# One plan between two scans: preparation beside the back stage, tiles of successive stages in shared slabs of SBUF

## The chip, the cores and the metric

The kernel runs on one core of a Trainium2 chip. The metric is device time in microseconds (us), the median of three runs. Engines are named as in the profile: PE is TensorE, DVE is VectorE, ACT is ScalarE, POOL is GpSimd, and SP is the engine whose queue issues all DMAs of this kernel.

## The reference

A batch of 8 images of 96 channels and 64 x 64 positions passes two layers. The first is a group norm, then a selective scan ("VSS") block with a residual; the second is linear attention and a quantized feed-forward block on 4096 tokens of 96. Cut to what matters:

```python
xh = layernorm(gn(x))                      # per position over 96 channels
xi, z = split(xh @ in_proj_w.T + in_proj_b)    # 192 and 192 channels
xi = silu(depthwise_conv3x3(xi) + conv_b)
xs = stack([xi_hw, xi_wh, flip(xi_hw), flip(xi_wh)])    # 4 directions k
dts, Bs, Cs = split(einsum('bkdl,kcd->bkcl', xs, x_proj_w), [6, 22])
delta = softplus(einsum('bkrl,kdr->bkdl', dts, dt_proj_w) + dt_proj_b)
# scan over 4096 positions, 16 states per channel:
h = exp(delta_t * A) * h + (delta_t * u_t) * B_t ;  y_t = sum_n h * C_t
y = layernorm(sum of the 4 directions, turned back) * silu(z)
x = x + y @ out_proj_w.T + out_proj_b
t = tokens(x)
t = t + linear_attention(layernorm(t))     # (q k^T) v without softmax: k^T v first
t = t + ffn(layernorm(t))                  # 96 -> 384 -> 96, operands rounded to fp8
```

## The kernel before

Images are worked in four pairs. For a pair the stages are:

- **project**: load x, statistics, group norm and layer norm, the input projection. Its output goes to three padded tiles `y` in SBUF (T = 0 and 1 hold 128 channels of either image, T = 2 the other 64 of both), and `zs` (silu of z) to DRAM. 16 chunks of 512 positions, 8 for each image.
- **convolve**: the 3 x 3 convolution from `y` to `xi`; T = 0 and 2 on DVE (lines 473 and 476), T = 1 on PE with diagonal weights (line 483), then Silu on ACT.
- **prepare**: for 2 orders (row-major, column-major), 8 chunks and 2 directions: x_proj on PE (line 543), dt_proj (line 555), softplus on ACT, `du` on DVE (line 560), and delta in three bf16 parts `dp` (ACT, DVE line 571, POOL line 576). `us`, `du`, `dl`, `bs` and `cs` are written to DRAM. Column-major chunks are first copied by POOL (line 535).
- **scan**: 128 steps of 128 positions (32 for each of the 4 directions), loaded from DRAM; it writes `ys`. A separate, hand-ordered program that the change leaves alone.
- **back**: 16 units. Load `ys` (tile `yk`), add directions (line 866 on DVE and POOL), turn by PE (line 880), layer norm (line 899), gate with `zs`, output projection, residual to `ta`, its normalized form to `tns`; keys and values (line 931) and their products summed in the bank `pm` (line 938). `ta` and `tns` are stored to DRAM as `t1` and `tn`. After the last unit the 96 x 96 attention matrix `hm` of each image is made.
- **tail**: 16 units. Load `tn` and `t1`, apply `hm` (line 985), layer norm, two fp8 products (lines 993 and 1004) and the output (line 1012). It needs `hm`, so it can't begin before back's last unit.

`norm` (lines 357, 361, 365) is the layer norm that project, back and tail share: a centering matmul into a bank of the ring `hold`, a square, a matmul into a bank of `q`, Ln and Exp on ACT, and a multiply on DVE which frees the `hold` bank. Nearly all ACT instructions are recorded at line 332 and all these DMAs at line 351.

**The order** of these stages is not that of the code. Every operation is added to a `Plan` with its engine, an assumed cost, the names that it reads and writes, the rings of tiles or PSUM banks that it needs a place of, and a `rank`. `Plan.run` then plays a schedule: for each engine it takes, among the operations that could begin within 0.1 us of the earliest, the one of least rank, and emits the earliest of these. A DMA is played on one queue of 0.23 MB/us. The instructions of each engine stand in the program in that order, and an engine runs them in order. Rings `unit` and `chunk` with three places limit how many units of back or tail and how many chunks of project are under way. Two plans run between scans: back of the last pair with project of the next (banks: 3 `q`, 2 `hold`, 2 `py`, and `pm`), then tail of the last pair with convolve and prepare of the next (3 `q`, 1 `hold`, 4 `big`). Their pools of SBUF are opened and closed with the plan. Before the first scan there is no back or tail, after the last one nothing else.

Constants are loaded ahead of everything, at the head of SP's queue, and `decay_weights()` (from line 285 on: an Exp, splits on DVE, four 128 x 6144 products at line 317, and DMAs to and from DRAM) stands between the first two plans.

Of the kernel before, what the change touches and what calls it, by code (L numbers as in the profile page):

```python
# [19 lines left out]
DIM = 96  # L20
# [17 lines left out]
HQ = TC // 4  # L38
NE = 24
# [12 lines left out]
class Plan:  # L52
# [9 lines left out]
    def __init__(self):  # L62
        self.ops, self.wrote, self.read = [], {}, {}
        self.free, self.left, self.tiles, self.home = {}, {}, {}, {}
        self.unit = None
# [7 lines left out]
    def add(self, engine, cost, emit, reads=(), writes=(), new=(), rank=0.0, kind=None, size=0.0):  # L73
        i = len(self.ops)
        after = set()
        for name in reads:
            after.update(self.wrote.get(name, ()))
            self.read.setdefault(name, []).append(i)
# [78 lines left out]
def vss_attn_ffn(ctx: ExitStack, tc: tile.TileContext, a: dict):  # L157
# [19 lines left out]
    gmat = load("gmat", [DIM, DIM])  # L177
    c96 = load("c96", [DIM, DIM])
    j96 = load("j96", [DIM, DIM])
    hmask = load("hmask", [DIM, DIM])  # L180
    j192 = const.tile([DIM, DIM], F32, name="j192")
    nc.sync.dma_start(j192, a["j192"][0:DIM, 0, 0:DIM])


    nw = load("nw", [DIM, 1])
    nb = load("nb", [DIM, 1])
    inb = const.tile([128, 2], F32, name="inb")
    nc.sync.dma_start(inb, a["inb"][:, 0])
    convw = load("convw", [128, 2, 9])
    convb = load("convb", [128, 2])  # L190
    dtb = load("dtb", [128, KD, 2])


    xwd = dram.tile([128, KD, 3, 76], F32, name="xwd", bufs=1)
    with tc.tile_pool(name="xprep", bufs=2) as wp:
        xw = wp.tile([128, KD, 3, 76], F32, name="xw", bufs=1)
        for k in range(KD):
            for g in range(2):
                xg = wp.tile([128, 3, 2 * NS], F32, name="xg")
                nc.sync.dma_start(xg, a["xw"][k, :, g, :, 0:32])  # L200
                for b in range(2):
                    o = 32 * g + NS * b
                    nc.vector.tensor_copy(
                        xw[:, k, :, o : o + NS].rearrange("p t (n z) -> p t n z", z=2),
                        xg[:, :, NS * b : NS * b + NS].rearrange("p t (z n) -> p t n z", z=2),
                    )
            nc.sync.dma_start(xw[:, k, :, 64:76], a["xw"][k, :, 0, :, 32:44])
        nc.sync.dma_start(xwd, xw)

    def cut(name, v, *rest):  # L210

        t = const.tile([DIM, 2, *rest], F32, name=f"c_{name}")
        nc.sync.dma_start(t[:, 0], v[0:DIM, 0])
        nc.sync.dma_start(t[0:32, 1], v[DIM:128, 0])
        nc.sync.dma_start(t[32:DIM, 1], v[0:64, 1])
        return t
# [5 lines left out]
    inz = const.tile([128, 2], F32, name="inz")  # L222
    for o in (0, 64):
        nc.sync.dma_start(inz[o : o + 64, 0:1], a["inb"][0:64, 1, 0:1])
    nc.sync.dma_start(inz[0:64, 1:2], a["inb"][64:128, 1, 0:1])
    nc.sync.dma_start(inz[64:128, 1:2], a["inb"][0:64, 1, 1:2])
    outb = load("outb", [DIM, 1])
    wkv = load("wkv", [DIM + 1, 2 * DIM])
    wqT = load("wqT", [DIM, DIM + 1])
    wff = load("wff", [DIM, DIM])  # L230
    bff = load("bff", [DIM + 1, DIM], part=slice(DIM, DIM + 1))


    dsum = const.tile([DIM, 2], F32, name="dsum")
    nc.vector.tensor_reduce(dsum, ds, mybir.AxisListType.X, ALU.add)
    ad = dram.tile([3, KD, DI, NS], BF16, name="ad", bufs=1)
    awd = dram.tile([KD, 128, 48 * 128], BF16, name="awd", bufs=1)

    blk = const.tile([128, 16], F32, name="blk")
    nc.sync.dma_start(blk, ident[0:16, 0:16].unsqueeze(1).to_broadcast([16, 8, 16]))  # L240


# [4 lines left out]
    with tc.tile_pool(name="wprep", bufs=1) as wp:  # L247
        w1 = wp.tile([DIM, HID], F32, name="w1")
        nc.sync.dma_start(w1, a["w1T"])
        nc.vector.tensor_copy(w1q, w1, saturate=False)  # L250
        w2 = wp.tile([128, 3, DIM], F32, name="w2")
        nc.sync.dma_start(w2, a["w2T"])
        nc.vector.tensor_copy(w2q, w2, saturate=False)
        b1 = wp.tile([128, 3], F32, name="b1")
        nc.sync.dma_start(b1, a["b1"])
        b18 = wp.tile([128, 3], F8, name="b18")
        nc.vector.tensor_copy(b18, b1, saturate=False)
        nc.vector.tensor_copy(b1q, b18)
        b2 = wp.tile([DIM, 1], F32, name="b2")
        nc.sync.dma_start(b2, a["b2"])  # L260
        b28 = wp.tile([DIM, 1], F8, name="b28")
        nc.vector.tensor_copy(b28, b2, saturate=False)
        nc.vector.tensor_copy(b2q, b28)
# [18 lines left out]
    def decay_weights():  # L282

        with tc.tile_pool(name="aprep", bufs=1) as wp:
            am = wp.tile([128, KD, 2, NS], F32, name="am")
            nc.sync.dma_start(am, a["alog"])
            nc.scalar.activation(am, am, AF.Exp)  # L290
            nc.vector.tensor_scalar(am, am, -1.0, None, ALU.mult)
            for i in range(3):
                ap = wp.tile([128, KD, 2, NS], BF16, name=f"ap{i}")
                nc.vector.tensor_copy(ap, am)
                if i < 2:
                    nc.vector.tensor_tensor(am, am, ap, ALU.subtract)
                for k in range(KD):
                    nc.sync.dma_start(ad[i, k, 0:128], ap[:, k, 0])
                    nc.sync.dma_start(ad[i, k, 128:DI], ap[0:64, k, 1])
            mask = wp.tile([128, 16], F32, name="mask")  # L300
            for p in range(3):
                nc.sync.dma_start(
                    mask[32 * p : 32 * p + 32],
                    ident[0:16, 0:16].unsqueeze(1).to_broadcast([16, 2, 16]),
                )
            for p in range(2):
                nc.sync.dma_start(mask[96 + 16 * p : 112 + 16 * p], ident[0:16, 0:16])
            for k in range(KD):
                ac = wp.tile([128, NE * NS], BF16, name="ac", bufs=2)
                for i, rows, n in ((0, slice(0, 96, 2), 6), (1, slice(1, 96, 2), 6), (2, slice(96, 128), 4)):  # L310
                    nc.sync.dma_start(
                        ac[rows],
                        ad[i, k].rearrange("(s c) n -> s (c n)", s=8).unsqueeze(0)
                        .to_broadcast([n, 8, NE * NS]),
                    )
                aw = wp.tile([128, 48, 16, 8], BF16, name="awp", bufs=2)
                nc.vector.tensor_tensor(
                    aw,
                    ac.rearrange("p (c n) -> p c n", n=8).unsqueeze(2).to_broadcast([128, 48, 16, 8]),
                    mask.unsqueeze(1).unsqueeze(3).to_broadcast([128, 48, 16, 8]), ALU.mult,  # L320
                )
                nc.sync.dma_start(awd[k], aw.rearrange("p c m n -> p (c m n)"))

# [30 lines left out]

    def norm(P, n, src_, read, dst, written, new, hold, rank, **kw):

        mm(P, 0.9, lambda: nc.tensor.matmul(P["ncp" + n][:DIM], c96, src_(), start=True, stop=True),  # L357
           (read,), ("ncp" + n,), (("ncp" + n, hold),), rank)
# [4 lines left out]
           ("nsq" + n,), ("nvp" + n,), (("nvp" + n, "q"),), rank)  # L363
# [5 lines left out]
    def project(P, pair, zs, ybuf, p1):  # L369

        pad = [t.rearrange("p (h w) -> p h w", w=HH + 2) for t in ybuf]
        for T in range(3):
            for edge in (pad[T][:, 0], pad[T][:, HH + 1], pad[T][:, :, 0], pad[T][:, :, HH + 1]):
                P.add("POOL", 0.4, lambda edge=edge: nc.gpsimd.memset(edge, 0.0), (), (f"edge{T}",))
        winT = p1.tile([DIM, 2 * DI], F32, name="winT")
# [4 lines left out]
        ring(P, p1, "xt", 2, [DIM, L])  # L380
        ring(P, p1, "zt", 2, [128, 2, F])
        P.ring("chunk", [None] * 3)
# [4 lines left out]
        for b in range(2):  # L387
            mv, gm, gd, gv, gr = stat[b]
            X, S = f"xt{pair}.{b}", f"stat{b}"
            k0 = b * 10 / 20  # L390
            for c in range(0, NCH, 2):
                cs = slice(c * F, c * F + 2 * F)
                dma(P, 0.4, lambda X=X, cs=cs: P[X][:, cs], lambda b=b, cs=cs: x[2 * pair + b, :, cs],
                    (), (f"{X}#{c}", f"{X}#{c + 1}"), ((X, "xt"),), k0 - 1)
            for c in range(NCH):
                dve(P, 0.67, lambda b=b, c=c, X=X: nc.vector.bn_stats(
                    bst[b][:, c, :], P[X][:, bass.ts(c, F)]), (f"{X}#{c}",), (f"{S}#{c}",), (), k0)
# [4 lines left out]
                P[g][:DIM, 0:1], gmat, mv[:, 0:1], start=True, stop=True), (S + "a",), (g,), ((g, "q"),), k0)  # L402
# [6 lines left out]
                P[v][:DIM, 0:1], gmat, gv, start=True, stop=True), (S + "v",), (v,), ((v, "q"),), k0)  # L409
# [7 lines left out]
            for c in range(NCH):  # L417
                cs = bass.ts(c, F)
                rank = k0 + (c + 2) / 20
# [4 lines left out]
                    P[X][:, cs], P[X][:, cs], gm, gr, ALU.subtract, ALU.mult),  # L424
                    (S + "r", S + "m"), (xc,), (), rank)
                norm(P, n, lambda X=X, cs=cs: P[X][:, cs], xc, lambda X=X, cs=cs: P[X][:, cs], (xc,), (),
                     "hold", rank)
                dve(P, 0.66, lambda X=X, cs=cs: nc.vector.tensor_scalar(
                    P[X][:, cs], P[X][:, cs], nw, nb, ALU.mult, ALU.add), (), (xc,), (), rank)
# [3 lines left out]
                    P[pm], winT[:, 0:128], P[X][:, cs], start=True, stop=True),  # L433
# [391 lines left out]
    def back(P, pair, ys, us, zs, t1, tn, tmp, psm):  # L825
        tns = ring(P, tmp, "tns", 3, [DIM + 1, F])
        for i, t in enumerate(tns):
            nc.gpsimd.memset(t[DIM : DIM + 1], 1.0)
# [358 lines left out]
```

## Time and profile before

| | |
|---|---|
| median of 3 runs (lowest, highest) | 10556.45 us (10539.96, 10565.98) |
| the profiled execution: its time, its span | 10552.56 us, 10550.8 us |
| busy in the span: PE, DVE, ACT, POOL | 7647.5, 9068.0, 6962.8, 7996.9 us |
| DMA | 2095.56 MB, mean 199 GB/s |
| scan steps begin and end, first scan | 638.9 us, 2414.6 us |
| scan steps begin, second, third, fourth scan | 3228.7, 5821.8, 8417.2 us |
| last scan step ends | 10192.6 us |

The profile is one execution. "Busy" is the time in which an engine had an instruction under way; a row of a group gives line, engine, operation, what it writes and reads, the count, the busy time and the mean of one. A stage's table gives the same busy times for one stretch, then the share of PE's clock that was granted, the busy share of the 16 DMA engines, and what they moved. Between scans of different pairs the program passes through stages with different limits, so the stretch has to be chosen before the row is read.

### The profile page before, as it was taken

What the parts mean: (1) busy time and instruction counts of PE and PEld (TensorE: products, weight loads), DVE (VectorE), ACT (ScalarE), POOL (GpSimd) and SP (SyncE); (2) the same over time, 40 slices, a digit from 0 to 9 for tenths busy, and PEclk for the clock granted to TensorE, in tenths of its full rate; (3) what the DMA queues carried; (4) which work ended last, traced back from release to release, by engine and by line L of the source; (5) the groups of instructions that cost most, each with busy time, mean ns of one, the idle gap of its engine ahead of it and who ended that gap; (6) DMA issues with size and microseconds to landing.
All of it is one profiled execution on the core that took longest, in us unless ns stands there. A gap on an engine that the chain in (4) does not pass through costs nothing. (4 is left out here: it accounts for less than half of the span.)

```text
span 10550.8 us, 377529 instructions
## 1 busy us (share of the span) xinstructions
PE 7647.5 (72%) x163328; PEld 5376.1 (51%) x163328; DVE 9068.0 (86%) x6702; ACT 6962.8 (66%) x12201; POOL 7996.9 (76%) x2802
## 2 busy tenths in 40 slices
PE   6766666668985676666987666776698666666678
PEld 2235555555324565555532555665553255555554
DVE  3689999996668999999566999999857699999985
ACT  3567777775566777776656677777665577777754
POOL 0579999992148999999124999999812599999961
PEclk8679999999878989999987889889897799989999
DMA  2787888879478888787947888888775778787885
GB/s 75 203 212 212 217 214 214 217 212 203 123 192 213 214 214 216 211 218 192 210 131 194 213 214 215 214 214 215 195 181 159 192 213 216 213 215 215 214 200 138
DMA packets 1597751, 2095.56 MB, mean 199 GB/s; under 512 B 407603, under 2 KB 1048116, under 8 KB 1592500
## 3 DMA queue, kind: packets, MB, share of 16 engines
q1 hardware_dynamic: 1596084, 2071.39, 75.6%
q8 instruction: 1283, 21.02, 0.9%
q14 instruction: 384, 3.15, 0.1%
HBM read 1606.82 MB, written 464.01 MB: 196 GB/s over the span
## 5 line engine op out<-in xcount | busy, mean ns | idle before, releaser
L743 DVE TENSOR_TENSOR_SCAN h<-da,dbu 128x774 f32<-128x774 f32 x4096 | 7026.7, 1759 | 128.2 <-POOL dbu L707 43.4
L707 POOL TENSOR_TENSOR dbu<-dut,bc 128x1536 f32<-128x1536 f32 x2048 | 7083.5, 3601 | 60.8 <-DMA dm<-dl 42.4
L732 ACT ACTIVATE da<-da 128x768 f32<-128x768 f32 x4092 | 3260.2, 797 | 1985.0 <-PE da L725 1970.1
L725 PE MATMUL da<-dm,aw 128*128 128x128 bf16 x24576 | 2282.4, 235 | 2329.8 <-DVE h L743 2089.6
L725 PEld LDWEIGHTS <-aw 128*128 128x128 bf16 x24576 | 1793.6, 104 | 2574.9 <-issue 2287.7
L761 PE MATMUL yp<-h,cw 128*32 128x48 f32 x131072 | 2902.4, 238 | 78.7 <-issue 65.7
L761 PEld LDWEIGHTS yp<-h,cw 128*32 128x32 f32 x131072 | 2410.2, 154 | 527.2 <-issue 207.0
L661 ACT ACTIVATE cw<-bc,blk 128x512 f32<-128x512 f32 x2048 | 1472.6, 720 | 81.5 <-DMA dm<-dl 81.5
L576 POOL TENSOR_TENSOR dp<-rest,dp 128x512 bf16<-128x512 f32 x384 | 456.8, 1194 | 665.3 <-ACT dp L332 620.0
L866 POOL TENSOR_TENSOR yd<-yk 128x768 f32<-128x768 f32 x64 | 125.6, 1962 | 779.6 <-DMA yk<-ys 407.1
L535 POOL COPY u<-xi 128x512 f32<-128x512 f32 x96 | 205.3, 2153 | 534.4 <-ACT xi L332 502.1
L555 PE MATMUL big<-S,dtw 12*128 12x512 f32 x768 | 521.1, 805 | 120.2 <-ACT d L332 96.0
L769 ACT ACTIVATE yev<-yp 128x384 f32<-128x384 f32 x1024 | 505.6, 494 | 64.5 <-PE yp L761 64.2
L571 DVE TENSOR_TENSOR rest<-d,dp 128x512 f32<-128x512 f32 x384 | 345.0, 904 | 207.6 <-ACT dp L332 161.2
L332 ACT ACTIVATE dp<-rest 128x512 bf16<-128x512 f32 x384 | 239.2, 628 | 304.6 <-DVE rest L571 303.5
L704 ACT COPY dbu<-h 128x12 f32<-128x12 f32 x1984 | 409.3, 206 | 0.0
L555 PEld LDWEIGHTS big<-S,dtw 12*128 12x128 f32 x768 | 157.7, 231 | 439.0 <-ACT d L332 225.7
L332 ACT ACTIVATE small<-hold 96x512 f32<-96x512 f32 x192 | 113.8, 593 | 313.5 <-PE hold L357 295.8
L560 DVE TENSOR_TENSOR du<-d,u 128x512 f32<-128x512 f32 x192 | 210.1, 1102 | 118.9 <-ACT d L332 118.9
L880 PEld LDWEIGHTS py<-ident,yd 128*96 128x96 f32 x2048 | 245.4, 165 | 91.2 <-issue 83.9
L476 DVE SCALAR_TENSOR_TENSOR xi<-y,c_convw,xi 128x2048 f32<-128x2048 f32 x128 | 290.3, 2347 | 0.0
L483 PE MATMUL big<-y,diag 128*128 128x512 f32 x576 | 260.2, 615 | 18.3 <-ACT xi L332 12.5
(122 smaller groups left out, 6009.5 us busy)
## 6 DMA issues: line engine op xcount, KB each, us to landing
dut<-du SPq DMA_DIRECT2D x2048, 384.0 KB
dm<-dl SPq DMA_DIRECT2D x1024, 288.0 KB
dl<-dp SPq DMA_DIRECT2D x256, 384.0 KB
dm<-dl SPq DMA_DIRECT2D x1024, 96.0 KB
ys<-yev SPq DMA_DIRECT2D x1024, 96.0 KB
du<-du SPq DMA_DIRECT2D x256, 256.0 KB
bc<-cs SPq DMA_DIRECT2D x512, 128.0 KB
bc<-bs SPq DMA_DIRECT2D x512, 128.0 KB
```

What stands on the lines that cost most here:

```text
L332: "ACT", cost, lambda: nc.scalar.activation(dst(), src_(), func, **kw),
L555: mm(P, 1.0, lambda pq=pq, k=k, T=T, S=S: nc.tensor.matmul(P[pq], dtw[64:76, k, T], P[S][64:76], start=True, stop=True), (S, "dtw"), (pq,) ...
L571: dve(P, 0.88, lambda rest=rest, d=d, dp=dp, w=w: nc.vector.tensor_tensor(w(rest), w(d), P[dp][:, :, 0], ALU.subtract), (d, dp + "#0"), (r ...
L576: P.add("POOL", 1.24, lambda rest=rest, dp=dp, w=w: nc.gpsimd.tensor_tensor(P[dp][:, :, 2], w(rest), P[dp][:, :, 1], ALU.subtract), (rest, ...
L661: nc.scalar.activation(cw[i % 2][:, :, :, m, :].rearrange("p z j t -> p (z j) t"), bc[i][:, 1].rearrange("p z (j t) -> p (z j) t", j=NB), ...
L704: nc.scalar.copy(start, segs(hs[s - 1][:, :, r])[:, :, :, 1 if back else TC])
L707: nc.gpsimd.tensor_tensor(segs(t)[:, :, :, 1:], dut[g].unsqueeze(1) .to_broadcast([128, 2, NI, TC]), bc[s // NB][:, 0, :, bass.ts(c % NB, ...
L725: nc.tensor.matmul(e[:, i], aw[k, r][:, i, z, :], dm[s // 2][:, NI * r + i, bass.ts(c % 2, TC)], start=True, stop=True,)
L732: nc.scalar.activation(e, e, AF.Exp)
L743: nc.vector.tensor_tensor_scan(hs[s][:, w, r][:, d], da[p % 3][:, o : o + W6][:, d], dbu[4 * s + r][:, w][:, d], 0.0, ALU.mult, ALU.add,)
L761: nc.tensor.matmul(y[32 * q : 32 * q + 32, 2 * NE * i : 2 * NE * i + 2 * NE] .rearrange("p (j r i) -> p i j r", j=2, r=NR), w[:, z, :, t], ...
L769: nc.scalar.activation(yev[s][:, :, o : o + 8, :].rearrange("p j i e -> p i j e"), y[:, 0 : 16 * NE].rearrange("p (i j e) -> p i j e", j=2 ...
```

## The change

- `decay_weights` and the loads of constants become rows of the first plan (function `weights`, with ranks); what used to be read freely (`c96`, `nw`, `inb` and so on) becomes a name that an operation reads. The four products move from DVE to POOL.
- The two plans between scans become one. Its banks are 3 `q`, 2 `hold`, 2 `py` and `pm`; before the first scan 4 `q` and 4 `hold`. The x_proj product and the PE part of convolve take a bank of `py` (`hold` before the first scan), dt_proj one of `q`.
- Ranks are rescaled: project 0 to 0.22, convolve to 0.28, prepare from 0.24 to 1, back 0 to 0.65, tail 0.54 to 0.65.
- A `Slab` is one SBUF tile that stages cut up in turn: project's tiles and then `xi` in A1, the padded `y` and then prepare's tiles in A2 (A3, after the weights, before the first scan). While `P.also` is set, each operation added reads that slab's name, and `gate_off` adds a row that writes it, so the plan puts the next user after it. That row emits no instruction.
- Tail takes its tiles from back's `yk` and `yd`. After the last scan, `ta` and `tns` stay in SBUF, and tail reads them there.
- Before the first scan five chunks of project may be under way (was three), with 10 `small` tiles (was 8). With back, `small` has 5 (was 6, and 4 for tail).

```diff
-    gmat = load("gmat", [DIM, DIM])
+    later = []
+    def lay(out_, in_, rank, name, after=()):
+        later.append((out_, in_, rank, name, after))
+    gmat = load("gmat", [DIM, DIM], -0.9)
...
+    class Slab:
+        def __init__(self, pool, name, size):
+            self.all, self.at = pool.tile([128, size], F32, name=name), 0
...
+    def weights(P, wp):
+        P.also = "A3"
+        for out_, in_, rank, name, after in later:
+            dma(P, 0.1, lambda out_=out_: out_, lambda in_=in_: in_, after, (f"w_{name}",), (), rank)
...
-                nc.vector.tensor_tensor(
-                    aw,
+            pool(14.0, lambda n=n, w=w: nc.gpsimd.tensor_tensor(
...
-        P.ring("chunk", [None] * 3)
+        P.ring("chunk", [None] * (3 if beside else 5))
...
-            k0 = b * 10 / 20
+            P.also = f"A1.{b}"
+            k0 = FRONT * b / 2
...
+    def gate_off(P, name):
+        P.add("SP", 0.0, lambda: None, (), (name,), rank=-9)
...
-                        start=(t == 0), stop=(t == 8)), (f"diag#{t}",), (n,), ((n, "big"),), -2 + h)
+                        start=(t == 0), stop=(t == 8)), (f"diag#{t}", "edge1", *[f"pad1#{j}" for j in range(NCH)]), (n,), ((n, "py" if beside else "hold"),), first)
...
-                rank = (o * NCH + c) / 16
+                rank = PREP + (1 - PREP) * (o * NCH + c) / 16
...
-                           (un[T], "xw"), (pt,), ((pt, "big"),), rank)
+                           (un[T], "xw"), (pt,), ((pt, "py" if beside else "hold"),), rank)
...
-                           (S, "dtw"), (pq,), ((pq, "big"),), rank)
+                           (S, "dtw"), (pq,), ((pq, "q"),), rank)
...
-            rank = i / 16
+            rank = BACK * i / 16
...
+            if kept is None:
+                dma(P, 0.2, lambda b=b, cs=cs: t1[b, :, cs], lambda ta=ta: P[ta], (ta,), (f"t1.{b}.{c}",), (), rank)
+                dma(P, 0.2, lambda b=b, cs=cs: tn[b, :, cs], lambda to=to: P[to][0:DIM], (to,), (f"tn.{b}.{c}",), (), rank)
...
-            rank = i / 16
+            rank = TAIL + i / 16 * (TAIL_END - TAIL) if kept is None else 1 + i / 16
...
+            if new and old:
+                psum = banks(P, st, q=3, hold=2, py=2)
+            elif new:
+                psum = banks(P, st, q=4, hold=4)
+            else:
+                psum = banks(P, st, q=3, hold=2, py=2)
+            ring(P, tmp, "small", 5 if old else 10, [DIM, F])
...
+                spare = back(P, pair - 1, old["ys"], old["us"], old["zs"], old["t1"], old["tn"], tmp, psum, kept)
+                tail(P, pair - 1, old["t1"], old["tn"], spare, kept)
+            if new:
+                for b in range(2):
+                    gate_off(P, f"A1.{b}")
+                A1.at = 0
+                xi = [A1.tile([128, L]) for T in range(3)]
+                convolve(P, xi, ybuf, tmp, bool(old))
...
+                prepare(P, A2, xi, new["us"], new["dl"], new["du"], new["bs"], new["cs"], bool(old))
+                P.also = None
+            P.run(table)
```

## The prediction

> **What bounds the kernel now.** I read the span by stage first, because the page's shares average stages with different limits. The four scans take 1776 us each (scan steps L743 from 638.9 to 2414.6 us, and so on); POOL and DVE are busy 1768 and 1757 us of that. Their code isn't touched. What the change can move is the rest, 3446 us: one stage before the first scan (639), three between scans (814, 816, 818) and one after the last (358). Rows of the stage table: interval and length, then busy us (and instructions) of PE, PEld, DVE, ACT, POOL, then granted clock, DMA share, GB/s.
>
> ```profile
> 0.00:638.90 638.90, 427.00 (x714) 136.75 (x715) 342.12 (x349) 305.16 (x499) 194.04 (x142) 0.75 0.57 152
> 2414.60:3228.70 814.10, 687.68 (x2186) 299.05 (x2187) 504.83 (x643) 479.48 (x780) 226.19 (x174) 0.82 0.72 179
> ...
> 10192.60:10550.80 358.20, 296.56 (x1472) 165.65 (x1472) 189.38 (x328) 143.32 (x258) 53.91 (x38) 0.93 0.69 160
> ```
>
> A middle stage is two plans, one after the other. Cut in slices of 27 us it has four regimes with different limits:
>
> ```profile
> 2523.10:2550.20 27.10, 27.10 (x126) 16.05 (x125) 15.96 (x24) 17.59 (x27) 5.04 (x2) 1.00 1.03 233
> ...
> 2740.20:2767.30 27.10, 27.10 (x65) 11.96 (x64) 27.10 (x13) 7.66 (x12) 0.00 (x0) 1.00 0.09 39
> ...
> 2848.70:2875.80 27.10, 26.11 (x40) 7.65 (x39) 13.03 (x21) 16.75 (x29) 7.62 (x6) 0.63 0.64 174
> ...
> 3120.00:3147.10 27.10, 23.35 (x35) 6.65 (x34) 16.58 (x17) 16.01 (x29) 16.73 (x14) 0.66 0.87 223
> ```
>
> Back beside project: PE without a gap. Convolve: PE and DVE full, DMA at 39 GB/s, ACT idle. Prepare beside tail: nothing full, PE at clock 0.63. Prepare alone: DMA 0.87 at 223 GB/s. So PE and DMA are each the limit in turn, and each is idle in the other's turn.
>
> A busy PE overstates its work: a record lasts until the pipeline drains, so its work is the distance between starts. From the timeline of PE:
>
> ```profile
> 2567.34 1.88 PE L899 MATMUL q<-g,j 96*96 96x512 f32 x4
> 2569.06 1.02 PE L432 MATMUL q<-xt,winT 96*128 96x512 f32 x2
> ...
> 2574.15 0.50 PE L938 MATMUL pm<-kv 128*96 128x96 f32 x4
> 2574.49 0.84 PE L931 MATMUL q<-c_wkv,tns 97*128 97x192 f32 x4
> 2575.17 1.04 PE L880 MATMUL py<-ident,yd 128*96 128x128 f32 x8
> 2576.05 1.93 PE L899 MATMUL q<-g,c_woT 96*96 96x512 f32 x4
> ```
>
> 512 columns of f32: 1.72/4 = 0.43 us a record, two records a matmul; L880 0.88/8 = 0.11; L931 0.68/4 = 0.17; L938 0.34/4 = 0.085. Work of a middle stage at full clock: a back unit 32 x 0.11 + 12 x 0.43 (L899) + 8 x 0.17 + 8 x 0.085 + 4 x 0.43 (norm) = 12.5 us, 16 units 200; project 16 x 10 x 0.43 = 69; convolve 144 x 0.43 = 62; prepare 384 x 0.43 = 165; tail at most 16 x (6 x 0.43 + 6 x 0.38) = 78, with 0.38 the length of an L993 record. Together 574 of the 814 us.
>
> **What the Trainium skill says.** "TensorE: Matmul & The Clock Gate", Part 1: PE runs at half clock until it has been busy for some 3.4 us and falls back when idle. The trace agrees: clock 1.00 where PE has no gap, 0.63 in prepare, where eight L543 records in a row take 6.61 us (0.83 each, not 0.43). "Perfetto Trace Analysis", Optimization Strategy: where the most contended engine changes over time, interleaving the regimes can help; that is this change, and the slices above are that case. "ScalarE: Activation LUTs", What ACT_TABLE_LOAD costs: about 1283 ns and a drain of about 1380; the trace shows 1283 ns loads, no drain as a row of its own. "SBUF — State Buffer", Who interferes with whom: a DVE instruction with two SBUF inputs contends with one on POOL that reads SBUF. The trace fits: L535 takes 2.87 us in the first stage, 1.93 in the middle ones. I read what moves from the order in which the changed kernel's instructions stand.
>
> **First stage: -115 us.** Its parts now:
>
> ```profile
> 34.00:185.00 151.00, 101.63 (x168) 35.37 (x168) 37.84 (x78) 90.08 (x131) 0.00 (x0) 0.81 0.21 57
> 185.00:230.00 45.00, 32.67 (x72) 14.17 (x72) 26.14 (x4) 1.12 (x2) 0.00 (x0) 0.89 0.45 167
> 230.00:308.00 78.00, 54.64 (x104) 20.96 (x104) 77.53 (x37) 23.29 (x38) 31.63 (x1) 0.76 0.18 59
> 308.00:615.00 307.00, 235.80 (x352) 64.37 (x352) 188.30 (x197) 183.41 (x319) 149.87 (x120) 0.68 0.87 223
> ```
>
> (1) Ahead of these lie 34 us in which SP issues constants, some 0.45 us each, before x. Now winT, swap and x stand first, so statistics start at about 6: -28. The constants still cost SP the same; they stand before the zs stores, and the last row of inz, which Silu needs, is near place 72: 72 x 0.45 = 32 us, earlier than the first Silu now (60). (2) Project, 151 us: DVE waits 101 us for ACT's normalization there, with two hold banks and three chunks in flight. With four and five it can fall to PE's 102 or stay; I take 125: -26. The 20 table loads of this stage become 12. (3) The decay weights, 45 us between two plans (four products L317, 26.14 us on DVE, and their DMAs), move to POOL beside project: -45. Costed on POOL by L707 (3.565 us for 1536 columns): 6144 columns 14.3, four 57 us; at 1.5 times that (the L535 ratio) 86. Cover: POOL has nothing else before the first u copy (276 us now). The awd stores stand among the zs stores on SP; a late product holds these, then the two zt buffers, then ACT; and prepare's tiles lie in the weights' slab A3, so prepare can't begin before the last awd store. If that is late, this gain is lost. (4) Convolve: part of image 0 goes before project's end; 62 us of DVE work remain after it where 78 are now: -16. (5) Prepare stays at 307 us (DMA). Between -70 and -140.
>
> **A middle stage: -66 us.** Ahead of the first prepare matmul PE now has all of project (69), convolve (62) and about 8 of 16 back units (100): 231 us. Start-up as now: PE worked about 36 of the first 54 us (slices at 2414 and 2441), so 18 lost. After project, DVE has some 48 us of convolve while PE has 72, then Silu. Some 20 us more lost: the first prepare matmul at about 270 (now about 378), 250 to 300. From there PE has at most 8 x 12.5 + 165 + 78 = 343, DVE 323 of 524, ACT in the same proportion 325 of 527 (455 us of activations and 56 loads; 44 now, so 15 us more). None decides. DMA does: SP's order moves 140 MB, 43 before the first us store of prepare, 97 after. Rates seen: 194 GB/s from prepare's start to its end now (76 MB in 394 us; 175 while tail runs beside it), 229 with prepare alone, up to 260 for ys loads. I take 218: 445 us. With first stores 8 us after the matmul and the scan's start-up unchanged at 27 (from the last rest L571 to the first scan step): 270 + 8 + 445 + 27 = 750, against 816. The convolve's DMA hole and the tail's slow stretch are what is gained. Ends: 200 GB/s gives 790, 240 GB/s 710. Costed at nothing: the P.also reads, which are rows of the plan and emit nothing; one more SP DMA; the boundary between the two plans (PE idle 6 of 27 us in the slice at 2713), inside the 18 and 20 lost. Next late: with prepare behind project in PE order, the SP queue. Each store waits at its head for POOL's dp (63.7 us of such waits now in 370), and behind it now wait back's yk loads, so back's start waits for prepare.
>
> **Last stage: -28 us.** Back's part (242 us, PE busy 217) is unchanged but for the 64 t1 and tn DMAs, which nothing waits for until tail. Tail:
>
> ```profile
> 10435.00:10550.80 115.80, 79.14 (x200) 28.51 (x200) 61.65 (x150) 62.03 (x112) 19.87 (x19) 0.87 0.27 82
> ```
>
> With one hold bank a unit's L357 starts only after the previous unit's L365: starts at 10443.67, 10451.15 and 10459.15 in the timeline, 7 to 8 us a unit, while ACT needs 62/16 = 3.9. Two banks and no reload: 5 us a unit, 80 for 107, and a few us at the boundary. Between -10 and -40.
>
> **Sum.** -115 - 3 x 66 - 28 = -341 from 10552.6 (span 10550.8 and 1.8 around it): 10212. The median of the three runs is 4 us higher, so I say 10215. Under 0.3% (32 us) a measurement here can't tell from no change.
>
> **Rivals.** A: DMA doesn't gain; stores at the head of SP's queue hold the loads, and the second part runs at today's 194 GB/s: 97/0.194 = 500, stage 805. With the first stage at -80 and the last at -15: 10552 - 80 - 33 - 15 = 10424. For it: SP's waits above, and both plans were paced by their order rather than by an engine. The case that slab tiles depend on each other, so that nothing overlaps, lands near: middle stages 0, 10552 - 115 - 28 = 10409; against it, the instructions' waits are fewer than before on every engine. B: everything fits; 240 to 250 GB/s and PE at full clock: 97/0.25 = 388, stage 693, -123 each: 10552 - 115 - 369 - 28 = 10040. C, slower: PSUM. Prepare's 96 softplus inputs had four banks of their own; now they share three q banks with back and tail, about 96 + 48 + 96 = 240 uses after the first prepare matmul. If a use holds its bank h us, this part takes 80h. At h = 6.4 a middle stage is 270 + 512 + 35 = 817, no gain; at 7.0 three stages lose 3 x 49 = 147 and eat the other gains, the point from which it decides; at 8, 270 + 640 + 35 = 945 and 10552 - 143 + 387 = 10796. Now a use is a matmul and an activation, 2 to 3.5 us, but ACT is in order and its longest wait inside prepare was 5.4 us.
>
> **How the numbers follow.** My case 0.55, A (with no overlap) 0.25, B 0.14, C 0.06. Range 10050 to 10440: it takes in A, nearly all of B, and leaves out C. Faster 0.94, same 0.01, slower 0.05.
>
> **What would show it.** First scan step near 524 (now 639); scans 1776 as before; middle stages 710 to 790 with no slice under 60 GB/s after the first 200 us, PE clock over 0.8 in prepare, the q users' waits short; tail's L357 starts 5 us apart at the end. It is wrong if middle stages stay over 800, if ACT or PE wait long for q banks, or if POOL's decay products hold the zs stores.

## The result, and the profile after

The changed kernel took **10456.25 us** (median of 4 runs, 10433.23 to 10467.46) against 10561.22 for the kernel before (median of 4): ratio 0.9902, interval 0.9887 to 0.9917. It is faster by about 1%; the prediction had 10215 and a range that began at 10050 and ended at 10440. The sign was right, the size was not: less than a third of the gain came.

The stage table says where it is missing (columns as before: interval, length, busy us and instructions of PE, PEld, DVE, ACT, POOL, then granted clock, DMA share, GB/s):

```profile
0.00:571.20 571.20, 422.44 (x714) 134.00 (x715) 339.47 (x340) 294.78 (x491) 225.81 (x152) 0.73 0.63 170
2348.50:3158.60 810.10, 707.73 (x2186) 302.13 (x2187) 489.98 (x644) 495.60 (x792) 216.57 (x172) 0.83 0.71 180
10116.10:10463.50 347.40, 299.56 (x1472) 165.12 (x1472) 191.75 (x329) 143.32 (x258) 57.19 (x34) 0.93 0.61 128
```

| stage (us) | before | predicted | after |
|---|---|---|---|
| first | 638.9 | 524 | 571.2 |
| middle, three | 814.1, 816.4, 818.2 | 750 | 810.1, 813.7, 810.1 |
| last | 358.2 | 330 | 347.4 |

First -68, the middle ones -4, -3 and -8, last -11: -93, and the four scans 6 us more in this execution (span 10463.5, was 10550.8). Of the 241 us between 10215 and 10456, some 184 are in the middle stages. Four slices of a middle stage, at the places that match those shown for the kernel before:

```profile
2402.50:2429.50 27.00, 27.00 (x102) 14.09 (x101) 15.19 (x24) 19.08 (x32) 3.77 (x2) 1.00 1.13 243
...
2564.50:2591.50 27.00, 27.00 (x65) 11.65 (x64) 25.86 (x14) 7.90 (x12) 0.00 (x0) 1.00 0.05 16
...
2672.50:2699.50 27.00, 23.07 (x43) 9.12 (x44) 13.35 (x16) 18.46 (x30) 9.83 (x8) 0.66 0.82 217
...
3077.50:3104.50 27.00, 23.03 (x33) 5.96 (x32) 14.96 (x27) 18.61 (x30) 7.52 (x5) 0.56 0.57 153
```

Back beside project is as before. Convolve still has a hole in DMA. What was to be new stands in the third and fourth row: prepare beside back, then beside tail. PE is at clock 0.66 and 0.56 there, busy for 23 of 27 us, while DMA is at 0.82 and then 0.57 and DVE, ACT and POOL are far from full. So no engine is full at its full rate; PE's time is nearly filled, at little more than half its rate.

Cut at the first prepare matmul (L594 starts at 2628.9), the stage falls into the two parts of the prediction:

```profile
2348.50:2628.50 280.00, 250.25 (x1095) 129.57 (x1096) 185.45 (x209) 157.86 (x240) 27.82 (x30) 0.94 0.68 155
2628.50:3135.50 507.00, 455.38 (x1076) 170.67 (x1074) 295.75 (x432) 331.99 (x542) 177.74 (x138) 0.79 0.73 191
```

First part 280 us, predicted 270 (250 to 300). Second part, up to the end of the last `rest` (L622), **507 us, predicted 453** (8 to the first stores and 445 of DMA), at 191 GB/s where 218 was taken. That is the miss: 54 of the 60 us by which a middle stage is longer than 750.

### The profile page after: what moved, and what is told of

Same layout as the page of the kernel before. It is cut to its first block, busy times and chain, and to the rows that moved or that the text cites. A ratio compares the mean times of both kernels' runs of the same rounds, so it can differ in the third digit from the quotient of the medians.

```text
span 10463.5 us, 377190 instructions
## 1 busy us (share of the span) xinstructions
PE 7723.3 (74%) x163328; PEld 5391.4 (52%) x163328; DVE 9031.7 (86%) x6692; ACT 6996.6 (67%) x12229; POOL 8006.9 (77%) x2799
## 5 line engine op out<-in xcount | busy, mean ns | idle before, releaser
L627 POOL TENSOR_TENSOR A<-A 128x512 bf16<-128x512 f32 x384 | 469.4, 1226 | 960.3 <-ACT A L287 940.3
L287 ACT ACTIVATE A<-A 128x512 bf16<-128x512 f32 (+2 forms) x809 | 486.2, 619 | 235.3 <-DVE A L622 229.9
L606 PE MATMUL q<-A 12*128 12x512 f32 x768 | 517.5, 786 | 57.2 <-ACT A L287 50.7
L622 DVE TENSOR_TENSOR A<-A 128x512 f32<-128x512 f32 x384 | 338.6, 887 | 206.0 <-ACT A L287 193.5
L586 POOL COPY A<-A 128x512 f32<-128x512 f32 x96 | 143.0, 1501 | 364.8 <-ACT A L287 318.7
L606 PEld LDWEIGHTS q<-A 12*128 12x128 f32 x768 | 147.3, 223 | 368.0 <-ACT A L287 209.0
L611 DVE TENSOR_TENSOR A<-A 128x512 f32<-128x512 f32 x192 | 188.4, 989 | 149.1 <-ACT A L287 148.6
L1073 POOL TENSOR_TENSOR yk<-yk,yd 96x512 f32<-96x512 f32 x64 | 89.7, 1404 | 294.4 <-DVE yd L1071 240.9
L937 PE MATMUL py<-ident,yd 128*96 128x128 f32 x2048 | 284.9, 291 | 24.7 <-DVE yd L923 11.2
L524 DVE SCALAR_TENSOR_TENSOR A<-A,c_convw,A 128x2048 f32<-128x2048 f32 x128 | 299.6, 2380 | 0.2
```

Source lines behind the costliest of these rows:

```text
L287: "ACT", cost, lambda: nc.scalar.activation(dst(), src_(), func, **kw),
L606: mm(P, 1.0, lambda pq=pq, k=k, T=T, S=S: nc.tensor.matmul(P[pq], dtw[64:76, k, T], P[S][64:76], start=True, stop=True), (S, "dtw"), (pq,) ...
L627: P.add("POOL", 1.24, lambda rest=rest, dp=dp, w=w: nc.gpsimd.tensor_tensor(P[dp][:, :, 2], w(rest), P[dp][:, :, 1], ALU.subtract), (rest, ...
L937: nc.tensor.matmul(o, P[yd][:, k, j, DIM * g : DIM * g + DIM], ident, start=(k + j == 0), stop=(k + j == 4),)
```

## The experiments

Two questions: what makes the second part long, and what lengthens the first stage. Stages are separated by scans, which nothing here touches, so an edit that acts in one stage is read in that stage. All are edits of the changed kernel except one; lengths are in us, "middle" is the mean of three, and the ratio is to the kernel before, with its interval.

| run | first | middle | last | median | ratio |
|---|---|---|---|---|---|
| after, first profile | 571.2 | 811.3 | 347.4 | 10456.25 | 0.9902 (0.9887, 0.9917) |
| after, again (c2) | 573.4 | 806.4 | 352.9 | 10460.06 | 0.9914 (0.9897, 0.9932) |
| e1, one ACT table | 570.6 | 793.3 | 345.7 | 10397.62 | 0.9851 (0.9836, 0.9866) |
| e2, 76 rows | 542.8 | 771.2 | 343.9 | 10314.41 | 0.9776 (0.9761, 0.9790) |
| e3, banks | 565.5 | 824.2 | 344.7 | 10492.26 | 0.9941 (0.9924, 0.9957) |
| e4, decay on DVE | 553.7 | 797.2 | 344.0 | 10422.91 | 0.9871 (0.9853, 0.9888) |
| e5, *before* with 76 rows | 638.3 | 794.6 | 355.9 | 10491.96 | 0.9947 (0.9932, 0.9962) |
| e6, 76 rows, DVE, tail banks | 516.8 | 768.8 | 365.3 | 10305.07 | 0.9771 (0.9757, 0.9786) |
| e7, 64 rows | 552.4 | 785.3 | 343.8 | 10364.98 | 0.9829 (0.9814, 0.9843) |
| e8, 128 rows, DVE | 519.6 | 755.7 | 347.2 | 10246.16 | 0.9705 (0.9688, 0.9721) |
| e9, 76 rows, DVE, one table | 512.8 | 749.0 | 343.9 | 10219.04 | 0.9683 (0.9664, 0.9701) |
| e10, 76 rows, DVE, more DMA | 535.5 | 776.7 | 346.9 | 10322.27 | 0.9776 (0.9759, 0.9793) |
| e11, 76 rows, DVE, POOL queue | 543.9 | 787.4 | 349.9 | 10361.61 | 0.9811 (0.9790, 0.9833) |
| e13, 76 rows, same order | 543.2 | 771.3 | 342.2 | 10310.73 | 0.9774 (0.9758, 0.9790) |
| e14, order of e8, 12 rows | 551.2 | 796.9 | 343.8 | 10429.98 | 0.9886 (0.9862, 0.9909) |

**The spread first.** 

> The changed kernel as it is, once more, beside the kernels below on their chip. Expected: 10456 us within 20, middle stages 810 to 814. It serves to read the stage lengths of this group against each other; a spread of more than 10 us in a middle stage between this profile and the first one would mean that stage differences of that size in single profiles carry nothing.

The same program gives middle stages of 801 to 814 us in two profiles; its second part was 495 us in the first middle stage of c2, at clock 0.81. Differences of 10 us in single profiles of kernels with 12 rows are therefore not read. e4 and e14, with 797 us, are such kernels too; the execution profiled was the fastest of their four, some 30 us below their medians.

**1. PE's clock in dt_proj.** dt_proj (L606) multiplies 12 rows of `S` by 12 rows of weights, where x_proj (L594) uses 128. These are the contraction rows: those over which the products are summed. Feeding it more rows with zero weights computes the same and takes the same number of columns.

```diff
+        dve(P, 0.8, lambda: nc.vector.memset(dtw[0:64], 0.0), (), ("dtwz",), (), -1)
...
-                            P[pq], dtw[64:76, k, T], P[S][64:76], start=True, stop=True),
+                            P[pq], dtw[0:76, k, T], P[S][0:76], start=True, stop=True),
```

> The changed kernel with dt_proj (L606) contracting over 76 rows of S instead of 12, the 64 more weight rows zero; same count, columns and result. Theory 'half clock': 12 rows count as little activity for the clock gate; with 76 PE's clock in the second part of a middle stage rises from some 0.77 to over 0.9 and the stage falls to 740-780. Theory 'table loads', 'PSUM banks' or 'SP queue', or a clock that only follows time busy: clock and stage as now, 805-815.

The middle stages fell by 40 us against the first profile after (35 against c2) and the whole by 142. The planner had moved some neighbours, since the zeroing is a row of the plan. So e13 issues the zeroing beside the load of the weights, and PE, ACT, POOL and SP keep the changed kernel's order row for row; e14 goes the other way, from the 128-row kernel below back to 12 rows with nothing else moved.

```diff
-        dma(P, 0.1, lambda: dtw[64:76], lambda
+        dma(P, 0.1, lambda: nc.vector.memset(dtw[0:64], 0.0) and dtw[64:76], lambda
```

> The changed kernel with 76 rows in the dt projection and the zeroing of the weights issued beside their load, so that PE, ACT, POOL and SP keep the changed kernel's order row for row. If the rows are the cause: as with 76 rows before, middle stages 765 to 775, first 540 to 548, total 10305 to 10335. If the planner's other order was the cause: middle 800 to 814, total 10440 to 10465.

```diff
-                            P[pq], dtw[:, k, T], P[S], start=True, stop=True),
+                            P[pq], dtw[64:76, k, T], P[S][64:76], start=True, stop=True),
```

> The kernel with decay products on DVE and 128 rows (middle stages 756, first 520, total 10246), with the contraction put back to 12 rows and every instruction left in its place, the zeroing too. If the rows are the cause: middle 795 to 812, first 548 to 558, total 10390 to 10435, clock in the second part 0.79 to 0.82. If the order was: middle 750 to 762, total 10240 to 10260.

The rows alone decide: e13 equals e2, and e14 gives back all three middle stages, 756 to 797. Matmuls whose rows were left alone got shorter as well. L1046, tail's first matmul, in the second part of the changed kernel and then of e13 (count, busy us, mean ns):

```profile
L1046 PE MATMUL q<-tns,hm 97*96 97x512 f32 x32 | 25.3, 894 | 0.4 <-ACT yd L287 0.4
```

```profile
L1046 PE MATMUL q<-tns,hm 97*96 97x512 f32 x32 | 19.6, 703 | 0.4 <-ACT yd L287 0.4
```

So it is the clock of all of PE that rose, not the speed of dt_proj alone.

How many rows, and whether their values matter, is what e7 (64 rows; the added inputs and weights are all zero) and e8 (128 rows) ask.

```diff
-                            P[pq], dtw[64:76, k, T], P[S][64:76], start=True, stop=True),
+                            P[pq], dtw[64:128, k, T], P[S][64:128], start=True, stop=True),
```

> The changed kernel with the dt projection contracted over the 64 rows from row 64 (12 as before, 52 with zero weights and zero inputs). Theory (the number of contraction rows in use decides whether these matmuls count as work for the clock, wherever they start and whatever they hold): clock in the second part of a middle stage near 0.87, middle stages 770 to 778, first stage 545 to 555, total some 10330. Rival (it was the start at row 0, or that the other rows held real B and C values instead of zeros): clock stays at 0.79 and middle stages at 800 to 814, total 10430 to 10460. In between (dose by rows): near 785.

> The changed kernel with the decay products on DVE and the dt projection over all 128 rows (zero weights in 116 of them, zero inputs in the 52 from row 76). Base, put together by stage from the runs of 76 rows and of DVE decay: first stage 517, middle 769, last 344, total 10284. Theory (dose by rows goes on: 12 rows 810, 64 rows 785, 76 rows 769 in a middle stage): clock in its second part over 0.90, middle 755 to 764, total 10240 to 10270. Rival (76 rows already give these matmuls their full effect; what half clock is left comes from PE's idle gaps): clock 0.88, middle 766 to 772, total 10275 to 10290.

The second part of a middle stage in the stage table, with 64, 76 (e13), 128 rows, and with 12 rows in e14. First e7:

```profile
2610.00:3092.80 482.80, 423.09 (x1074) 158.82 (x1072) 299.23 (x432) 331.78 (x542) 178.29 (x138) 0.85 0.75 201
```

e13:

```profile
2602.40:3067.40 465.00, 394.56 (x1072) 163.09 (x1072) 301.04 (x431) 330.46 (x542) 179.30 (x138) 0.89 0.78 209
```

e8:

```profile
2572.00:3029.50 457.50, 381.99 (x1117) 159.68 (x1115) 305.46 (x436) 334.91 (x548) 183.80 (x141) 0.93 0.81 216
```

e14:

```profile
2607.00:3105.50 498.50, 448.41 (x1108) 171.11 (x1106) 296.80 (x435) 336.02 (x548) 181.32 (x141) 0.81 0.74 198
```

Read the second number and the one before the DMA share together. With 12 rows (after, c2, e4 and e14), 64, 76 and 128 the clock is 0.79 to 0.81, 0.85, 0.89, 0.93, PE's busy time 455 to 442, 423, 395, 382, and the part 507 to 492, 483, 465, 457. Busy time times clock is an estimate of PE's work at full clock: 360 in the changed kernel, 360, 351, 355. It hardly moves, so the same work was done at another rate. DVE, ACT and POOL are busy for nearly the same time in each row; the GB/s rise because nearly the same bytes pass in less time. Zero rows count too. In the slices of e8 the clock reads 1.00 from 2647 to 2890 us, where after has 0.62 to 1.00 at the same place of its stage.

Was this cost there before the change? e5 is the kernel *before* with 76 rows, all else in its order.

> The kernel before, with the dt projection contracted over 76 rows instead of 12 (64 of them with zero weights); the order of all instructions is kept. Theory (PE's half clock in prepare comes from the 12-row matmuls whatever else stands beside them, and prepare is slowed by it in the kernel before too): clock in prepare from 0.63-0.68 to over 0.75, middle stages 20 to 35 us shorter each, first stage 10 to 25 shorter, together some 95 us: 10465. Rival (in the kernel before prepare is paced by DMA, 0.87 at 223 GB/s, and only the merged plan made PE the limit): clock up, but stages within 10 us of 814-818 and 639, total 10530 to 10560. The first would say that the change moved no limit and that the 12-row matmul costs both kernels alike; the second that the merge put PE's half clock on the path.

Its part from the first prepare matmul on, in the kernel before and in e5:

```profile
2792.00:3205.50 413.50, 335.13 (x576) 103.81 (x574) 261.74 (x348) 272.30 (x460) 179.75 (x136) 0.72 0.72 189
```

```profile
2794.00:3184.50 390.50, 299.17 (x577) 100.85 (x575) 260.29 (x348) 271.70 (x460) 179.81 (x136) 0.79 0.76 201
```

Each expectation held in one place. In this part the clock rose from 0.72 to 0.79 and the middle stages fell by 22 us, so prepare was slowed by it before the change too; in the first stage, where prepare stands alone at 223 GB/s, the time stayed (638.3) though the clock rose there too (0.71 to 0.77 from 220 to 547 us). The merge nearly doubled what the 12 rows cost: 35 to 40 us for 22. Put the other way, merging gains 5 to 10 us a middle stage with 12 rows (816 to 811 and 806), 23 with 76 (795 to 771). The ratios of the medians, less what the first and last stages gained, say the same: an estimate of 7 to 8 us with 12 rows, 25 with 76.

**2. Is DMA the limit of the second part?** e10 stores `dl` of tile 0 a second time into a spare buffer. The last line of the diff is the added transfer.

```diff
+    def twice(P, size, out_, in_, more, reads, rank):
+        def emit():
+            nc.sync.dma_start(out_(), in_())
+            nc.sync.dma_start(more(), in_())
```

> The changed kernel with 76 rows and decay on DVE, and with each dl store of tile 0 issued a second time into a spare buffer: 32 x 393 KB = 12.6 MB more for every pair, no other work, the order of all else kept. Base 517, 769, 344, total 10284. If DMA now paces prepare, as the prediction costed it (97 MB at 218 GB/s), every byte counts: at 210 GB/s 60 us more in each middle stage and at 230 GB/s 55 in the first, total 10515. If the stage is paced by the in-order chains of the engines and DMA has slack (its mean share was 0.78), under 15 us more in a middle stage; in the first stage, where prepare stands alone at 231 GB/s, 30 to 55; total 10320 to 10385.

The middle stages (781.5, 778.6, 770.0) took 8 us more in the mean than those of e6 for 12.6 MB, where 60 were to come if DMA paced them. The second part of the longest:

```profile
2590.00:3073.00 483.00, 414.38 (x1110) 171.17 (x1108) 300.93 (x434) 336.42 (x548) 182.93 (x141) 0.85 0.83 231
```

It moves 231 GB/s here, 40 more than in the changed kernel and 22 more than in e6 (209), at a lower clock (0.85 for 0.88): DMA had room. For 128 rows, at 216 GB/s, the question was not asked. In the first stage, with prepare alone, 19 us more; there it is nearer to the limit, though short of the 30 to 55 expected.

**3. SP's queue (rival A).** e11 lets POOL issue the `dl` stores, right behind the product they wait for.

```diff
-                               (dp + "#0", dp + "#1", dp + "#2"), (), rank)
+                               (dp + "#0", dp + "#1", dp + "#2"), (), rank, "gpsimd")
```

> The changed kernel with 76 rows and decay on DVE, and with the dl stores issued by POOL behind the product that they wait for, instead of by SP; nothing else is moved. Base 517, 769, 344, total 10284. Theory of rival A of the prediction (stores waiting at the head of SP's queue hold back the loads of back and tail behind them): the waits of SP for POOL go (29 waits, 35 us in 270 us of the second part), the second part gets 10 to 25 us shorter, middle 745 to 760, total 10220 to 10255. Against it: the loads are early enough anyway, middle 766 to 772. POOL's own issue can cost: 128 issues for a pair; at 1 us each POOL would be busy some 310 of 467 us, and the stage slower, 775 to 800.

Slower, by its second ground. From the groups of POOL in the second part (line, operation, count, busy us, mean ns, idle before):

```profile
L628 POOL TENSOR_TENSOR A<-A 128x512 bf16<-128x512 f32 x95 | 117.0, 1236 | 153.2 <-ACT A L287 147.3 <-DMA cs<-A 4.6
L306 POOL DMA_DIRECT2D dl<-A x126 | 96.9, 772 | 15.1 <-POOL A L628 14.2 <-issue 0.3 <-DMA dl<-A 0.3
```

126 issues cost POOL 97 us. Whether a queue without these waits would help is not told apart from that cost. What argues against rival A is e13: SP's order stayed, and so did most of its waits for POOL's `dp` (62 us for 75), yet the part fell by 42 us. A smaller share of A is not excluded.

**4. Table loads and PSUM banks.** e1 and e9 replace Softplus and Silu by Exp, so that ACT loads one table in all; their output is another.

```diff
-        if kind == "ln" and loaded[0] != "ln":
+        if loaded[0] is None:
...
+        func = AF.Exp if func in (AF.Softplus, AF.Silu) else func
```

> The changed kernel with Softplus and Silu replaced by Exp (that part of the result is changed), so that one activation table serves everything: the 179 table loads within the stages go, in the same order of instructions. Theory 'table loads' (56 loads of 1.28 us on ACT per middle stage delay every chain that passes ACT): middle stages fall from 810 to 740-770. Theory 'PE at half clock is the bound', 'PSUM banks' or 'order of SP's queue': 795-810, since ACT has 8 us in 27 to spare.

> The changed kernel with 76 rows, decay products on DVE, and Exp in the place of Softplus and Silu, so that ACT loads one table in all; the output is another for that. Base 517, 769, 344, total 10284. With 12 rows the same swap took 13 to 20 us from a middle stage. If the table loads are a loss of their own (ACT held 1.28 us and its consumers behind it), they come off again: middle 749 to 755, total 10225 to 10240. If PE's low clock and ACT's loads were one loss seen twice, because only the slower of the two chains counts, middle 764 to 770, total 10270 to 10290.

e1's 13 to 18 us lie near the spread of 12-row kernels. e9 settles it: 20 us come off each middle stage on top of the rows, 4 off the first. Loads are a loss of their own (56 in a middle stage, 44 before). Second part of e9:

```profile
2565.50:3014.50 449.00, 387.52 (x1077) 162.88 (x1075) 301.44 (x432) 283.78 (x507) 179.38 (x138) 0.89 0.81 216
```

e3 spreads dt_proj's output over three rings.

```diff
-                           (S, "dtw"), (pq,), ((pq, "q"),), rank)
+                           (S, "dtw"), (pq,), ((pq, ("q", "hold", "py")[T] if beside else "q"),), rank)
```

> The changed kernel with dt_proj's bank taken from q, hold and py in turn (by T) instead of always q, between scans. Theory 'PSUM banks' (240 uses of three q banks after the first prepare matmul): middle stages fall by 30 us or more. Otherwise: the order changes, the bound does not; 800-830, with hold and py now short for the others.

13 us slower in a middle stage. The order changes with it, so this shows only that more places for these inputs don't help as the planner uses them; rival C has no support.

**5. The first stage.** Its parts after: project, the rest of convolve, prepare.

```profile
6.00:160.00 154.00, 90.41 (x153) 32.43 (x154) 98.96 (x115) 69.54 (x109) 45.69 (x10) 0.73 0.35 106
160.00:220.00 60.00, 58.28 (x135) 24.26 (x135) 56.96 (x27) 27.23 (x42) 27.18 (x2) 1.00 0.31 101
220.00:547.00 327.00, 271.57 (x411) 75.42 (x410) 176.59 (x197) 190.56 (x330) 140.14 (x118) 0.69 0.82 210
```

Project takes 154 us, not 125, up to about DVE's last norm multiply (155 us; the last of project's matmuls end at 169, beside convolve). The timeline of POOL and then that of DVE around 66 us (start, length, line, operation):

```profile
62.94 21.51 POOL L385 TENSOR_TENSOR A<-A 128x6144 bf16<-128x6144 bf16 x2 [35.06 <-DMA A<-ad]
88.48 10.90 POOL L385 TENSOR_TENSOR A<-A 128x6144 bf16<-128x6144 bf16 x1 [4.03 <-DMA A<-ad]
```

```profile
65.99 7.74 DVE L442 TENSOR_TENSOR A<-A 96x1 f32<-96x1 f32 x1
73.76 10.70 DVE L444 SCALAR_TENSOR_TENSOR A<-A 96x1 f32<-96x1 f32 x1
84.39 0.15 DVE L331 TENSOR_REDUCE dsum<-c_ds 96x2 f32<-96x8 f32 x1
...
89.16 12.33 DVE L461 TENSOR_SCALAR A<-A 96x512 f32<-96x512 f32 x5 [0.41 <-ACT A L287]
```

Two operations on one column each take 7.74 and 10.70 us: they end as POOL's two decay products do, at 73.7 and 84.5. A third product stands beside L461. e4 and e6 put these products back on DVE, in the same plan.

```diff
-            pool(14.0, lambda n=n, w=w: nc.gpsimd.tensor_tensor(
+            dve(P, 6.6, lambda n=n, w=w: nc.vector.tensor_tensor(
```

> The changed kernel with the four decay products (128 x 6144) on DVE as rows of the plan, as they were on DVE before, instead of POOL. Theory 'POOL holds the SBUF port and DVE stands': DVE's small operations of 10.7 us in the first stage go back to 0.15-0.53, and the first stage falls from 571 by 15 to 40 us though DVE has 26 us more work. Theory 'SP's constants and awd loads delay project': first stage within 10 us of 571. Middle stages 810 in both.

L461 in the changed kernel and in e4 (min/median/max ns, first and last start):

```profile
L461 DVE TENSOR_SCALAR A<-A x16: 529/532/10504, 14.4 to 147.0; 96x512 f32<-96x512 f32 x16
```

```profile
L461 DVE TENSOR_SCALAR A<-A x16: 533/536/542, 15.2 to 123.2; 96x512 f32<-96x512 f32 x16
```

The 10.5 us case is gone, the last start is 24 us earlier, and the stage is 17 us shorter. e4's median lies some 35 us below after's; the rest lies in stages whose plan the edit doesn't touch, and with a range of 39 us in its four runs that is left as the spread of 12-row kernels.

**6. The last stage.** e6 also gives tail's first fp8 product the two `py` banks.

```diff
-                    P[p1], w1q[:, bass.ts(m, 128)], P[tq], start=True, stop=True), (tq,), (p1,), ((p1, "q"),), rank)
+                    P[p1], w1q[:, bass.ts(m, 128)], P[tq], start=True, stop=True), (tq,), (p1,), ((p1, "q" if kept is None else "py"),), rank)
```

> The changed kernel with three edits that act in different stages: the dt projection over 76 rows (zero weights in 64), the decay products on DVE in the same plan (first stage only), and in the tail of the last stage the w1 products in the two py banks instead of the three q banks. Expected by stage: first, if POOL's products and the half clock are separate losses, 543 - 17 = 526 (predicted blind: 524); if they hide the same time, 540. Middle 769 as with the 76 rows alone. Last: if the three q banks hold the tail's units back, 6 us a unit becomes 5 and the stage falls from 344 to some 330; if the units wait for their own chains of ACT and DVE, it stays at 344. Sum with both gains 10280, with neither 10314.

First 517, below even the 526 of two separate losses; middle 769; last 21 us *longer*. Starts of tail's first matmul (two records each for 16 units) in the kernel before, after, and e6:

```profile
L985 PE MATMUL q<-tf,hm x32: 590/594/1140, 10440.2 to 10531.6; 97*96 97x512 f32 x32
```

```profile
L1046 PE MATMUL q<-kept,hm x32: 590/593/1062, 10363.9 to 10444.9; 97*96 97x512 f32 x32
```

```profile
L1047 PE MATMUL q<-kept,hm x32: 590/592/1169, 10175.9 to 10272.3; 97*96 97x512 f32 x32
```

Over 15 steps that is 6.1, 5.4 and 6.4 us a unit. In e6's waits in the tail (who waits for whom: us in total, times, longest) ACT waits for the next unit's `hold` product, and that for a DVE addition:

```profile
ACT small L287 <- PE hold L394: 42.9, 16, 9.2
PEld hold L394 <- DVE yk L1049: 35.8, 15, 3.0
```

With other banks the planner's order changed too, and set the units nearly one behind the other. So this doesn't show what the `q` banks cost in the old order, only that freeing them did not bring the units closer. What order would bring 5 us was not tried.

**The best version** that computes the reference is e8: 10246.16 us, 0.9705 of before (0.9688, 0.9721), three times the change's own gain.

## Why the prediction was wrong, step by step

- **Middle stage, first part: right.** 280 us for 270.
- **Middle stage, second part: the step that failed.** "From there PE has at most ... 343 ... None decides. DMA does." Both halves are refuted. 343 us was work at full clock; at the 0.79 that was granted it is 434 (an estimate), and PE was busy 455 of 507 us; with nearly the same bytes to move, 128 rows in dt_proj took the part to 457. The prediction had read the clock of 0.63 in prepare and then priced PE without it, even though it had eight L543 records in 6.61 us. Its test "PE clock over 0.8 in prepare" states the assumption; the slices of prepare beside tail have 0.56 to 0.84. That a busier PE would lift its own clock was taken from the Trainium skill's account ("TensorE: Matmul & The Clock Gate", Part 1), and "the trace agrees" was a misreading: the slice with 0.63 has PE busy for 26.11 of 27.10 us. After the merge PE was busy for 90% of the second part, where it had been for 81% of the part from the first prepare matmul on, and the clock was 0.79 for 0.72.
- **218 GB/s** was the wrong kind of price: a rate seen in a stage is what its engines let through, and nearly the same bytes passed at 191 to 216 GB/s as the rows changed, at 231 with more bytes. With 128 rows the part is 457 us and with one table (at 76 rows) 449, against 453 forecast. The hole in convolve's DMA, which was counted as gained, is still there: 16 GB/s in a slice 216 us into the stage, where none under 60 was to come after 200.
- **Table loads**: 15 us of ACT were seen and put beside other work; e9 gives 20 us a middle stage for all of them, so PE alone does not set the pace. What part is owed to the 12 more loads was not measured.
- **First stage, -68 for -115.** Constants -28 as forecast; the separate stretch of the weights (-45) gone; convolve 60 us left for 62. Project +3 for -26, and prepare 327 for 307: 49 us together, against the 47 missed. Two steps fail. "Cover: POOL has nothing else" asked who waits for POOL, and put the price of the shared reads on POOL alone (14.3 us, times 1.5). POOL took 10.8 us; DVE paid, 17 us of the stage (e4). "Prepare stays at 307 us (DMA)" left out the clock, which took another 28 (e2). With both mended (e6) the stage is 517, near the 524 forecast, but partly by luck: prepare is then some 290 us for 307, project and convolve together some 197 for 187.
- **Last stage, -11 for -28.** The unit time was nearly right, 5.4 us for 5, but there was less to gain: the kernel before had 6.1 over all 16 units, not the 7 to 8 read from three starts. The sum was not right either: 16 x 5 leaves out the run-out, 18.6 us from the last unit's start to the end, of which one step of 5 was counted. Back's part stayed (248 us before and after).
- **Rivals.** A's numbers came nearest (second part at 194 GB/s, stage 805, total 10424), but not by A's mechanism: with SP's order kept (e13) the part is 42 us shorter. A number that fits does not carry its cause. B's 240 to 250 GB/s was reached in no second part that was measured; the most was 231, with more bytes. C has no support. Under "shows it wrong" the prediction named middle stages over 800, and POOL's products; that they would hold DVE rather than the stores was not among them.

## What to carry to other kernels

Price work at the clock that the stage shows, not at the one that another stage has: where PE is "busy" and nothing else is full, PE may be the limit at half rate, and then filling it with more work gains little. If one of its matmuls contracts over few rows, padding it with zero rows is a cheap trial: the columns and the result stay. A rate of DMA read in a stage is a limit only if more bytes cost time there; doubling one store is a cheap test. When work moves to an idle engine, ask what its reads do to the neighbour that shares its port, not only who waits for its result.

## What the runs showed of the hardware

- Granted clock and contraction rows. The Trainium skill ("TensorE: Matmul & The Clock Gate", Part 1) ties the half clock to how busy PE has been. Here PE was about 90% busy at clock 0.79; with dt_proj over 64, 76 and 128 rows instead of 12 it was granted 0.85, 0.89 and 0.93, while it was 88%, 85% and 83% busy. The number of rows fed counts, also where they hold zeros. By what measure the chip counts it is not shown.
- POOL beside DVE. "SBUF — State Buffer", Who interferes with whom, in the Trainium skill says that a DVE instruction with two SBUF inputs contends with POOL's reads, and that the ports they share are an exclusive lock. The trace agrees: 7.74 and 10.70 us for operations on one column of 96 partitions, ending with the products of 10.8 us. L461, with one wide input and two of one column, was held too: 10.50 us for 0.53.
- A DMA issued by POOL took 0.77 us of POOL's time (126 issues, 96.9 us, in e11).
